# Unread products of the head with 128 columns in place of 256, and the steps of the first fourteen iterations in new places

## The chip, the cores and the metric

The kernel runs on one core of a Trainium2 chip. A core has five engines that work side by side, each from its own queue in strict order: TensorE (PE, matrix products, with a weight load for each), VectorE (DVE), ScalarE (ACT), GpSimd (POOL), and SyncE (SP), whose queue here only starts DMAs. Engines wait for one another by semaphores. The metric is the device time of one execution in microseconds.

## The reference

The reference is one layer of message passing on 128 graphs of 64 nodes with 128 features. For every pair of nodes (i, j) of a graph a three-layer network makes a message of the two nodes' features; the messages are multiplied by the adjacency matrix and summed over j; a second network of the same form updates each node.

```
messages = _mlp(concat[x_i, x_j], msg_w0, msg_b0, ..., msg_w2, msg_b2)   # for all pairs
messages = messages * adj[..., None]
agg      = sum(messages, axis=2)
updated  = x + _mlp(concat[x, agg], upd_w0, upd_b0, ..., upd_w2, upd_b2)
# _mlp: relu(x @ w0 + b0), layer norm, relu(@ w1 + b1), layer norm, @ w2 + b2
```

The adjacency matrix holds zeros and ones, some 12% ones and a full diagonal. So only the pairs with an edge matter.

## The kernel before, in words

The kernel works on edges alone. Each graph gets 640 slots for its edges (five tiles of 128). Two graphs make a pair p (0 to 63), four pairs a block b (0 to 15), two pairs a quad q (0 to 31) with five chunks of 512 edges; chunks are counted by n (0 to 159).

Per block, the place of each edge among the slots is found: `rank` (a scan along each row of the adjacency matrix, DVE), `count` (a product with a triangular matrix, PE), `count_out` and `degrees` (ACT), `place` and `place_out` (POOL; for block 0 `place_first` and `place_pair` on DVE and `place_rest` on POOL). Per pair, `distance` (ACT) and `make_tp` (DVE) mark the slots of each row node, `marks` (PE) and `compare` (DVE) the column node; `node_rows` (ACT for the first six pairs, then POOL) copies the row marks to float32. `stack(p,0)` and `stack(p,1)` are two DMAs each on SP's queue, which put row marks and column marks on top of each other in a tile S[p]. For pairs 0 and 1 no DMA is used: `rows_here` (ACT), `marks_here` (PE) and `compare_here` (DVE) write S directly. `node_marks(p)` is a transposing DMA on SP's queue.

`turn_x`, `turn_x_out`, `rows`, `rows_hi` and `rows_lo` make the first layer's products of each node (transposes and products on PE, copies on ACT, the low part on DVE or POOL).

Per chunk n: `gather(n)` (L946, PE) multiplies those node products by S, so that each edge gets its sum; `relu0(n)` (L951, ACT); `turn_h(n)` (L956, PE, four transposes); `stats0(n)` (L613, DVE); `seed(n)` (ACT or POOL, the second layer's bias times the deviation); `layer1(n)` (L1003, PE); `relu1(n)` (DVE or ACT); `stats1(n)` (DVE). `root_of`, `root1_of`, `inverse_of`, `var1_step` finish the norms per quad, `weights` and `reduce_block` sum the edges into nodes, and the node network follows per block.

gather(n) reads columns 512n to 512n+511 of the slots, so gather(5) is the first to need S[2], gather(7) S[3], gather(15) S[6]. There is one PSUM bank for gather's result, so gather(n+1) waits until relu0(n) is done.

`ahead`, `keep` and unnamed steps derive folded weights once, in the first iterations.

The order of all this is written out by hand. `at(n, place, fn, ...)` files a step under an iteration n and one of sixteen places within it; the table MOVE (lines 24 to 356) overrides that: for a key such as `"gather@@5"` (gather of iteration 5) it gives a shift of the iteration, a new place, and a rank within it. Negative iterations hold the steps of the head, with a running number: `"count@@-1#6"`. At the end all steps run in order of iteration, place and rank, and each step's instructions go to the end of their engines' queues. Changing MOVE therefore changes the order of each engine's queue and nothing else. Tile semaphores follow from the data that steps read and write.

`keep_busy(k)` writes products that nobody reads: `mean_m` against itself (128 columns) k times if k is above 4, else `mean_m` against `first` (256 columns) k // 2 times. It is called with k = 7 once, 4 three times and 2 seven times, so that there are 13 products of 256 columns and 7 of 128. Each float32 product is two records in the trace.

Of the kernel before, what the change touches and what calls it, by code (L numbers as in the profile page):

```python
# [24 lines left out]
    "<lambda>@@1": (1, "s", 1), "<lambda>@@10": (-1, "m", -1), "<lambda>@@11": (0, "T", 2),  # L25
    "<lambda>@@2": (1, "x", 2), "<lambda>@@3": (1, "S1", -1), "<lambda>@@4": (1, "k", 2),
    "<lambda>@@5": (0, "k", 2), "<lambda>@@6": (-1, "S1", -1), "<lambda>@@7": (-1, "T", 2),
    "<lambda>@@8": (0, "k", -5), "<lambda>@@9": (152, "L0", 3), "ahead@@0": (2, "x", 7),
    "ahead@@1": (2, "x1", -1), "ahead@@2": (1, "x1", 0), "ahead@@3": (2, "L1", -1),
    "ahead@@4": (1, "k", 3), "ahead@@6": (0, "T", 2), "bias0.@3": (-7, "a", 2),  # L30
# [3 lines left out]
    "compare.0@7": (0, "m", 0), "compare.0@@0": (2, "x", 6), "compare.0@@10": (2, "e0", 3),  # L34
    "compare.0@@12": (2, "s", 1), "compare.0@@140": (-2, "S1", -1),
    "compare.0@@142": (-2, "k", -1), "compare.0@@145": (-3, "T", 0),
    "compare.0@@147": (-2, "x2", 2), "compare.0@@150": (2, "s", -1),
    "compare.0@@152": (2, "m", -2), "compare.0@@2": (2, "b", 2), "compare.0@@5": (1, "S1", 1),
    "compare.0@@7": (1, "L0", 0), "compare.1@1": (2, "T", -3), "compare.1@3": (3, "y", 2),
    "compare.1@6": (0, "x2", 2), "compare.1@8": (1, "s", 1), "compare.1@@1": (2, "x", 5),  # L40
    "compare.1@@11": (2, "T", -3), "compare.1@@13": (3, "a", 4), "compare.1@@138": (-1, "S1", 1),
    "compare.1@@141": (-2, "T", -1), "compare.1@@143": (-1, "b", 1),
    "compare.1@@146": (-1, "x", 2), "compare.1@@148": (3, "x", 2), "compare.1@@151": (2, "e0", 3),
    "compare.1@@153": (3, "b", 4), "compare.1@@3": (2, "x1", -2), "compare.1@@6": (2, "a", -1),
    "compare.1@@8": (2, "S1", 2), "compare_here@@-1#26": (3, "s", 1),
    "compare_here@@-1#31": (3, "s", 1), "compare_here@@-1#41": (3, "k", 4),
    "compare_here@@-1#47": (3, "x", -1), "count@8": (-2, "e0", -3), "count@@-1#6": (0, "e", -9),
    "count@@1": (1, "k", 5), "count@@138": (-2, "S1", -6), "count@@8": (1, "s", -3),
    "count_out@9": (-3, "e0", -1), "count_out@@-1#7": (0, "e", -9),
    "count_out@@139": (-3, "x", -4), "count_out@@2": (0, "x", 0), "count_out@@9": (0, "e1", 3),  # L50
    "degrees@9": (-6, "T", -2), "degrees@@-1#11": (1, "a", -1), "degrees@@139": (-3, "s", -2),
    "degrees@@2": (0, "s", 2), "degrees@@9": (0, "x1", 0), "distance@0": (-4, "k", -3),
    "distance@3": (1, "k", -1), "distance@5": (-3, "x", -2), "distance@8": (-2, "b", 1),
    "distance@@-1#13": (1, "x2", 0), "distance@@-1#27": (1, "e1", 1),
    "distance@@-1#33": (3, "y", 2), "distance@@1": (1, "k", 4), "distance@@10": (-3, "a", 1),
    "distance@@13": (2, "e", 2), "distance@@138": (-2, "a", -1), "distance@@140": (-3, "s", -1),
    "distance@@143": (-5, "S1", -2), "distance@@145": (-2, "y", 3), "distance@@148": (-7, "k", -1),
    "distance@@150": (-1, "x", 2), "distance@@3": (2, "k", 5), "distance@@5": (1, "y", -3),
    "distance@@8": (0, "x1", -1), "finish.@8": (2, "s", -2), "finish.@@138": (0, "x", -2),
# [7 lines left out]
    "gather@@-1#28": (3, "y", 3), "gather@@-1#35": (3, "x1", -4), "gather@@-1#43": (4, "x", 1),  # L67
    "gather@@0": (3, "e0", 4), "gather@@1": (4, "L1", -5), "gather@@10": (1, "x2", -3),
    "gather@@11": (1, "e0", 3), "gather@@12": (2, "L1", -1), "gather@@13": (2, "e", 2),
# [7 lines left out]
    "gather@@159": (0, "e", 2), "gather@@5": (0, "x1", -1), "gather@@6": (0, "y", -2),  # L77
    "gather@@7": (0, "a", 0), "gather@@8": (0, "k", -6), "gather@@9": (-1, "x1", -1),
# [3 lines left out]
    "inverse_of@@165": (0, "m", 0), "inverse_of@@168": (2, "x2", -1), "keep@@1": (1, "x1", 0),  # L82
    "keep@@10": (0, "L0", 1), "keep@@2": (2, "b", -1), "keep@@3": (2, "L1", -6),
    "keep@@4": (1, "L1", -1), "keep@@5": (0, "k", 3), "keep@@6": (-1, "x1", -1),
    "keep@@7": (1, "s", -2), "keep@@9": (-1, "x1", 3), "keep_busy@@-1#0": (21, "x1", 0),
    "keep_busy@@-1#18": (3, "s", 1), "keep_busy@@-1#23": (17, "x2", -2),
    "keep_busy@@-1#30": (1, "e1", 1), "keep_busy@@-1#37": (17, "T", 2),
    "keep_busy@@-1#45": (3, "s", 1), "keep_busy@@-1#9": (17, "k", -5),
    "keep_busy@@2": (-3, "e", -7), "keep_busy@@3": (-4, "e", -3), "keep_busy@@4": (-5, "e", -7),
    "keep_busy@@5": (-4, "m", -1), "layer1@0": (-3, "m", -1), "layer1@1": (-2, "s", 1),  # L90
    "layer1@2": (-2, "e", 0), "layer1@3": (0, "b", -1), "layer1@4": (2, "m", 3),
    "layer1@5": (1, "y", 0), "layer1@6": (0, "L0", -3), "layer1@7": (-1, "k", -4),
    "layer1@8": (-2, "S1", -7), "layer1@9": (-2, "m", -1), "layer1@@10": (-1, "L1", 1),
    "layer1@@11": (1, "k", 0), "layer1@@12": (1, "e0", 0), "layer1@@13": (1, "L0", 3),
    "layer1@@138": (-2, "S1", -3), "layer1@@139": (-3, "x2", 2), "layer1@@140": (-3, "s", -2),
    "layer1@@141": (-4, "e1", 0), "layer1@@142": (-2, "m", 0), "layer1@@143": (-3, "S1", 2),
    "layer1@@144": (-2, "T", -1), "layer1@@145": (-3, "T", 0), "layer1@@146": (-3, "x", 0),
    "layer1@@147": (-3, "a", 1), "layer1@@148": (0, "a", 0), "layer1@@149": (1, "b", -2),
    "layer1@@150": (-1, "e1", -1), "layer1@@151": (1, "k", 2), "layer1@@152": (1, "T", -3),
    "layer1@@153": (1, "x", -2), "layer1@@154": (1, "m", -1), "layer1@@155": (1, "y", 8),  # L100
    "layer1@@157": (0, "y", -4), "layer1@@158": (0, "a", -2), "layer1@@159": (0, "x2", 1),
    "layer1@@160": (0, "x2", -2), "layer1@@161": (0, "L0", 3), "layer1@@162": (0, "T", -5),
    "layer1@@164": (1, "m", 1), "layer1@@165": (0, "b", 2), "layer1@@166": (0, "e0", 1),
    "layer1@@167": (-1, "m", -2), "layer1@@8": (-2, "e", 0), "layer1@@9": (-1, "k", -5),
    "layer_a.@6": (0, "T", 1), "layer_a.@@146": (3, "x", 2), "layer_a.@@156": (2, "x", -2),
    "layer_a.@@169": (-1, "x1", 0), "layer_a._0@@170": (4, "a", -2),
    "layer_a._2@@171": (7, "L1", 2), "layer_b.@1": (-1, "x1", 1), "layer_b.@@141": (0, "s", 3),
    "layer_b.@@151": (5, "a", 4), "layer_b.@@161": (4, "m", 0), "layer_b.@@171": (5, "y", 2),
    "layer_b._0@@172": (30, "s", 1), "layer_b._2@@173": (30, "s", -1), "layer_c.@7": (-1, "x2", 2),
    "layer_c.@@147": (6, "s", 1), "layer_c.@@157": (4, "s", 1), "layer_c.@@164": (2, "L1", 1),  # L110
    "layer_c.@@173": (30, "L0", 2), "layer_c._0@@174": (39, "x", 0),
    "layer_c._2@@175": (41, "y", -2), "layer_out..uh.m0@7": (-1, "k", -2),
    "layer_out..uh.m0@@147": (2, "e1", 2), "layer_out..uh.m0@@157": (2, "L1", 1),
    "layer_out..uh.m0@@170": (2, "x1", -1), "layer_out..uy.usdb@2": (1, "T", -2),
    "layer_out..uy.usdb@@142": (0, "L0", -4), "layer_out..uy.usdb@@152": (4, "b", 4),
    "layer_out..uy.usdb@@162": (3, "S1", -2), "layer_out..uy.usdb@@172": (5, "L0", -1),
    "layer_out._0.uh.m0@@171": (3, "s", -2), "layer_out._0.uy.usdb@@173": (30, "s", -2),
    "layer_out._2.uh.m0@@172": (7, "a", 2), "layer_out._2.uy.usdb@@174": (30, "k", -1),
    "load_adj@1": (-3, "s", 3), "load_adj@@-1#1": (0, "e", -8), "load_adj@@-1#3": (1, "e1", 2),
    "load_adj@@1": (1, "s", 1), "load_adj@@11": (-6, "a", -2), "load_x@8": (-3, "e0", 3),  # L120
    "load_x@@-1#2": (2, "a", 0), "load_x@@-1#4": (2, "m", -1), "load_x@@138": (-2, "T", -1),
    "load_x@@8": (-6, "x", 7), "make_tp@1": (-4, "m", 0), "make_tp@4": (2, "a", 2),
    "make_tp@6": (-2, "s", 1), "make_tp@9": (-3, "e0", -4), "make_tp@@-1#15": (2, "a", -1),
    "make_tp@@-1#32": (2, "e0", 1), "make_tp@@-1#46": (3, "k", 3), "make_tp@@1": (2, "x", 2),
    "make_tp@@11": (-3, "k", -2), "make_tp@@139": (-3, "x2", 3), "make_tp@@141": (-3, "x1", -3),
    "make_tp@@144": (-5, "k", -1), "make_tp@@146": (-3, "x", 3), "make_tp@@149": (-7, "S1", 1),
    "make_tp@@151": (1, "k", 3), "make_tp@@4": (1, "x1", 0), "make_tp@@6": (0, "k", 2),
    "make_tp@@9": (0, "L0", 4), "marks.0@0": (-1, "x2", 4), "marks.0@2": (2, "L0", 1),
    "marks.0@5": (1, "L0", -1), "marks.0@7": (-1, "e0", 0), "marks.0@@0": (2, "x", 0),
# [230 lines left out]
def tile_gnn(  # L360
# [40 lines left out]
    nc = tc.nc  # L401
# [85 lines left out]
    mean_m = const.tile([P, P], F32, name="mean_m")  # L487
# [1160 lines left out]
```

## Time and profile before

| | us |
|---|---|
| median of five runs | 503.92 |
| lowest and highest | 502.51 and 505.54 |
| the profiled execution | 502.7 |
| its span, first to last instruction | 500.9 |

| engine | busy us | share of the span |
|---|---|---|
| PE | 490.6 | 98% |
| weight loads (beside PE) | 467.6 | 93% |
| DVE | 460.7 | 92% |
| ACT | 398.1 | 79% |
| POOL | 354.3 | 71% |

Busy time of PE counts products from start to modelled end, and neighbours overlap; what a product costs in a full queue is read from the distance of its start to the next start. Idle time in a timeline stands in brackets, with what ended it. SP's rows are issues of DMAs, whose data land later (3.0 us in the median for `stack(p,0)`, 2.7 for `stack(p,1)`).

### The profile page before, as it was taken

Reading aid. Unit: us, or ns where it says so; the run is one execution under the profiler, and the core shown is the slowest. Engines: PE = TensorE matmul, PEld = TensorE weight load, DVE = VectorE, ACT = ScalarE, POOL = GpSimd, SP = SyncE. Lnnn points to the kernel's source line nnn. Section 1 sums busy time; section 2 is a strip of 40 time slices with the busy share of each in tenths; the row PEclk is TensorE's granted clock in tenths of the full one; section 3 lists DMA queues with packets and bytes.
Section 4 is the critical chain, followed back from the end, with each engine's and each line's share of the span. In section 5 each row is a group of like instructions: output and inputs, shape, how many; then the busy total and the mean of one; then the engine's idle time right before and its main releaser. Section 6 shows DMA issues by size and latency. Waiting matters only on the chain.

```text
span 500.9 us, 15934 instructions
## 1 busy us (share of the span) xinstructions
PE 490.6 (98%) x5969; PEld 467.6 (93%) x5969; DVE 460.7 (92%) x1225; ACT 398.1 (79%) x907; POOL 354.3 (71%) x563
## 2 busy tenths in 40 slices
PE   7999999999999999999999999999999999999995
PEld 5899999999999999999999999999999999999984
DVE  7899788999999999999999999899999989998885
ACT  6999978888787788968778897877879778867753
POOL 3277686877869687785968778696886669674941
PEclk9999999999999999999999999999999999999999
DMA  4769475658849575694956667475565647355201
GB/s 122 167 145 171 105 139 120 132 121 141 167 105 151 119 148 121 139 165 106 151 127 135 135 130 162 98 168 128 121 150 117 152 110 170 85 114 107 63 23 46
DMA packets 91474, 63.55 MB, mean 127 GB/s; under 512 B 57473, under 2 KB 75522, under 8 KB 91394
## 3 DMA queue, kind: packets, MB, share of 16 engines
q1 hardware_dynamic: 91106, 62.36, 58.9%
q8 instruction: 49, 0.80, 0.7%
q14 instruction: 31, 0.25, 0.2%
q10 hardware_dynamic: 288, 0.13, 0.1%
HBM read 7.15 MB, written 4.19 MB: 23 GB/s over the span
## 4 chain that ended last, share of the span: by engine, by line


## 5 line engine op out<-in xcount | busy, mean ns | idle before, releaser
L1003 PE MATMUL z<-w1c,h 128*128 128x128 f32 x1280 | 167.4, 275 | 0.0
L1003 PEld LDWEIGHTS z<-w1c,h 128*128 128x128 f32 x1280 | 158.1, 191 | 4.1
L613 DVE BATCH_NORM_STATS2 st<-hT 128x6 f32<-128x256 f32 x320 | 120.5, 418 | 21.6 <-PE hT L956 17.7
L951 ACT ACTIVATE h<-hps,b0c 128x512 f32<-128x512 f32 x160 | 109.6, 685 | 23.9 <-PE hps L946 22.7
L993 ACT ACTIVATE z<-b1b,m_sd 128x128 f32<-128x128 f32 x320 | 118.8, 371 | 11.6 <-DVE y L597 4.7
L613 DVE BATCH_NORM_STATS2 st<-y 128x6 f32<-128x256 f32 x320 | 118.1, 419 | 0.1
L989 POOL TENSOR_TENSOR u<-b1b,m_sd 128x512 f32<-128x512 f32 x80 | 82.8, 1044 | 29.4 <-ACT m_sd L621 28.9
L956 PE MATMUL hT<-ident,h 128*128 128x128 f32 x640 | 96.5, 273 | 0.7 <-ACT h L951 0.6
L946 PE MATMUL hps<-s,abl 128*128 128x512 f32 (+3 forms) x256 | 93.5, 371 | 0.8 <-DMA s<-j 0.5
L1045 POOL TENSOR_TENSOR w<-oh,m_q 128x192 f32<-128x192 f16 x126 | 62.6, 511 | 39.8 <-issue 27.0
L956 PEld LDWEIGHTS hT<-ident,h 128*128 128x128 f32 x640 | 74.3, 141 | 1.9 <-ACT h L951 1.0
L946 PE MATMUL hps<-s,abh 128*128 128x512 f32 (+3 forms) x256 | 74.3, 322 | 0.0
L1012 ACT ACTIVATE y<-z 128x512 f32<-128x512 f32 x80 | 47.4, 595 | 30.9 <-PE z L1003 30.7
L928 DVE TENSOR_TENSOR j<-mk,cmpt 128x320 fp32r<-128x320 f32 x124 | 58.4, 471 | 1.4 <-PE mk L920 1.2
L597 DVE CUSTOM_DVE_ANT_0 y<-z,u 128x512 f32<-128x512 f32 x80 | 54.0, 675 | 4.0 <-PE z L1003 2.4
L889 ACT ACTIVATE d<-slot,mid 128x640 f16<-128x640 f16 x64 | 52.7, 826 | 0.7 <-DVE mid L799 0.7
L946 PEld LDWEIGHTS hps<-s,abl 128*128 128x128 f32 x256 | 48.7, 190 | 2.8 <-DMA s<-j 0.7
L946 PEld LDWEIGHTS hps<-s,abh 128*128 128x128 f32 x256 | 48.5, 189 | 0.0
L1060 PE MATMUL ys<-y,w 128*32 128x128 f32 x1488 | 44.3, 274 | 0.0
L1060 PEld LDWEIGHTS ys<-y,w 128*32 128x32 f32 x1488 | 39.7, 110 | 3.6 <-POOL w L1045 2.6
L904 POOL CAST i<-tp 128x640 fp32r<-128x640 f16 x58 | 42.4, 746 | 0.0
L920 PE MATMUL mk<-tp,posall 128*128 128x320 f16 x126 | 37.9, 300 | 0.2 <-DVE j L928 0.2
(195 smaller groups left out, 852.2 us busy)
## 6 DMA issues: line engine op xcount, KB each, us to landing
s<-i SPq DMA_DIRECT2D x124, 160.0 KB, 3.0
s<-j SPq DMA_DIRECT2D x124, 160.0 KB, 2.7
xn<-in_x_dram SPq DMA_DIRECT2D x15, 256.0 KB, 4.0
out_dram<-uo SPq DMA_DIRECT2D x15, 256.0 KB, 2.5
an<-in_adj_dram SPq DMA_DIRECT2D x16, 128.0 KB, 2.7
oh<-tp SPq DMA_TRANSPOSE x64, 3.1
xn<-in_x_dram SPq DMA_DIRECT2D x2, 128.0 KB, 3.2
out_dram<-uo SPq DMA_DIRECT2D x2, 128.0 KB, 3.5
```

What stands on the lines that cost most here:

```text
L597: nc.vector._custom_dve(TENSOR_ADD_SAT, out=o, in0=ps, in1=sb, s0=BIG, s1=0.0)
L613: nc.vector.bn_stats(st, src.rearrange("p t c -> p c t"))
L889: nc.scalar.activation(D[p], slot, AF.Abs, bias=blocks[b]["mid"][:, q:q + 1], scale=-1.0)
L928: nc.vector.tensor_tensor(JR[p][:, c], MK.pop((p, k))[:, 0:HC], cmpt[:, c], op=ALU.is_equal)
L946: nc.tensor.matmul(ps[:, c:c + w], lhsT=ab[:, g % 4, :], rhs=s, start=(k == 0), stop=(k == 1))
L951: nc.scalar.activation(H[n], HP.pop(n), AF.Relu, bias=b0c)
L956: nc.tensor.transpose(ps[:, t, :], H[n][:, t * P:(t + 1) * P], ident)
L989: nc.gpsimd.tensor_tensor(U[n], bc(W["b1b"], CH), SR[q][:, k:k + CH].unsqueeze(2).to_broadcast([P, CH, C]), op=ALU.mult)
L993: nc.scalar.activation(z_of(n)[:, t, :], W["b1b"], AF.Copy, scale=SR[q][:, k + t:k + t + 1])
L1003: nc.tensor.matmul(ps[:, t, :], lhsT=h[:, t * P:(t + 1) * P], rhs=W["w1c"], start=added and t == 0, stop=True, skip_group_check=True)
L1045: (nc.vector if p == NP - 2 else nc.gpsimd).tensor_tensor(WT[p][:, g], oh, qs, op=ALU.mult)
L1060: nc.tensor.matmul(YS[b][g * N + m * HN:g * N + (m + 1) * HN, k, :], lhsT=w[:, g, m, u, :], rhs=y, start=(u == 0), stop=(u == TH - 1), til ...
```

## The change

Two things are changed. `keep_busy` uses 128 columns always, with the number of products as it was (13 and 7). And the entries of MOVE for the head and for iterations 0 to 13 have new values (some 570 positions of 2,983 in the order differ, nearly all before the step gather(19); of those behind it, keep_busy(7) and root_of(3) change places, and a step that issues no instruction moves). No step is added or removed.

```
-            if k > 4:
-                for _ in range(k):
-                    nc.tensor.matmul(warm[:, 0, :], lhsT=mean_m, rhs=mean_m, start=True, stop=True)
-            else:
-                for _ in range(k // 2):
-                    nc.tensor.matmul(warm[:, 0:2, :], lhsT=mean_m,
-                                     rhs=first.rearrange("p q j -> p (q j)"), start=True,
-                                     stop=True)
+            for _ in range(k if k > 4 else k // 2):
+                nc.tensor.matmul(warm[:, 0, :], lhsT=mean_m, rhs=mean_m, start=True, stop=True)
```

```
 MOVE = {
...
-    "compare.1@@11": (2, "T", -3), ...
+    "compare.1@@11": (4, "a", 2), ...
-    "count@@-1#6": (0, "e", -9),
+    "count@@-1#6": (1, "s", -1),
-    "keep_busy@@-1#0": (21, "x1", 0), "keep_busy@@-1#18": (3, "s", 1), "keep_busy@@-1#23": (17, "x2", -2),
-    "keep_busy@@-1#30": (1, "e1", 1), "keep_busy@@-1#37": (17, "T", 2), "keep_busy@@-1#45": (3, "s", 1),
-    "keep_busy@@-1#9": (17, "k", -5), "keep_busy@@2": (-3, "e", -7), "keep_busy@@3": (-4, "e", -3),
-    "keep_busy@@4": (-5, "e", -7), "keep_busy@@5": (-4, "m", -1),
+    "keep_busy@@-1#0": (21, "x1", 1), "keep_busy@@-1#18": (1, "y", 4), "keep_busy@@-1#23": (17, "e1", -2),
+    "keep_busy@@-1#30": (1, "e1", -3), "keep_busy@@-1#37": (17, "T", 1), "keep_busy@@-1#45": (2, "e1", -2),
+    "keep_busy@@-1#9": (1, "b", 0), "keep_busy@@2": (2, "k", 0), "keep_busy@@3": (-3, "s", -1),
+    "keep_busy@@4": (0, "s", -1), "keep_busy@@5": (11, "k", -5),
-    "node_marks@@9": (0, "x1", 4), "node_marks@@10": (-4, "e1", 3),
+    "node_marks@@9": (-5, "x1", -1), "node_marks@@10": (-5, "k", 10),
-    "node_rows@@10": (2, "e0", 4),
+    "node_rows@@10": (5, "e0", 3),
-    "stack.0@@11": (3, "x1", -1), "stack.1@@12": (4, "m", 5),
+    "stack.0@@11": (5, "L1", -2), "stack.1@@12": (3, "e0", 2),
...
```

The order that follows, from the first step to the step gather(5):

```
before
load_adj(0); rank(0); keep_busy(2); keep_busy(2); odd_weights(0); count(0); keep_busy(2); count_out(0); place_first(); degrees(0); distance(0); distance(1); keep_busy(4); load_adj(1); place_pair(0); make_tp(0); load_x(0); turn_x(0,0,2); rank(1); load_x(1); keep_busy(2); marks_here(0); turn_x_out(0,0,2); make_tp(1); rows_here(0,0); place_rest(); turn_x(0,2,4); load_adj(2); rows(0,0,0,2); keep_busy(4); compare_here(0,0); compare_here(0,1); keep_busy(2); turn_x_out_rest(); degrees(1); rows_hi(0,0,0,2); marks_here(1); distance(2); rows_lo(0,0,0,2); gather(0); make_tp(2); distance(3); rows(0,0,2,4); rows_here(0,1); relu0(0); compare_here(1,0); count(1); rows_hi(0,0,2,4); compare_here(1,1); turn_h(0); count_out(1); marks(2,0); rows_lo(0,0,2,4); compare(2,0); load_x(2); rows_here(1,0); ahead(); gather(1); keep(); stats0(0); marks(2,1); relu0(1); node_rows(2); rows_here(1,1); turn_h(1); gather(2); ... stack(2,0); stack(2,1); ... stack(3,0); compare(3,1); stack(3,1); gather(5)
after
load_adj(0); rank(0); odd_weights(0); degrees(0); load_adj(1); count(0); count_out(0); keep_busy(2); place_first(); distance(0); distance(2); keep_busy(2); load_x(0); place_pair(0); make_tp(0); keep_busy(4); turn_x(0,0,2); turn_x_out(0,0,2); distance(1); rank(1); marks_here(0); compare_here(0,0); rows(0,0,0,2); ahead(); turn_x(0,2,4); make_tp(1); rows_hi(0,0,0,2); rows_lo(0,0,0,2); rows_here(0,0); load_adj(2); keep_busy(4); turn_x_out_rest(); rows_here(0,1); compare_here(0,1); make_tp(2); place_rest(); gather(0); marks_here(1); relu0(0); rows(0,0,2,4); compare_here(1,0); distance(3); count(1); count_out(1); rows_hi(0,0,2,4); compare_here(1,1); gather(1); degrees(1); relu0(1); marks(2,0); rows_here(1,0); rows_here(1,1); compare(2,0); keep_busy(2); place(1); rows_lo(0,0,2,4); turn_h(0); gather(2); stats0(0); ... compare(2,1); ... load_x(2); gather(3); stack(2,1); ... node_rows(2); ... keep_busy(2); ... gather(4); ... keep_busy(2); ... relu0(4); ahead(); stack(2,0); node_marks(0); node_rows(3); ... node_marks(1); gather(5)
```

Further on, up to gather(15):

```
before
... node_rows(6); node_rows(7); ... stack(7,0); ... stack(6,0); ... node_marks(2); ... load_x(3); ... gather(13); ... stack(6,1); ... gather(15)
after
... seed(6); ... place_out(2); ... node_marks(2); ... stack(6,1); ... load_x(3); node_rows(6); ... stack(6,0); stack(7,0); ... gather(15)
```

In both versions the four products of keep_busy(4), keep_busy(2) and keep_busy(2) that stand in iteration 16, and keep_busy(7) in iteration 20, stay about where they were.

## The prediction

> **What bounds the kernel now.** I read the page first (engine sums, slices), then a table of busy time by stretch of time, then the timelines of TensorE (PE), ScalarE (ACT), VectorE (DVE) and of SP's queue up to 62 us, where the change lies.
>
> ```profile
> span 500.9 us, 15934 instructions
> PE 490.6 (98%) x5969; PEld 467.6 (93%) x5969; DVE 460.7 (92%) x1225; ACT 398.1 (79%) x907; POOL 354.3 (71%) x563
> ```
>
> ```profile
> 10.00:20.00 10.00, 9.35 (x100) 7.32 (x100) 9.51 (x26) 9.84 (x22) 2.81 (x6) 1.00 0.57 134
> 20.00:30.00 10.00, 9.52 (x99) 8.56 (x98) 8.29 (x22) 9.17 (x21) 5.17 (x5) 1.00 0.77 179
> 30.00:40.00 10.00, 10.00 (x126) 9.35 (x128) 9.95 (x25) 9.84 (x27) 6.88 (x11) 1.00 0.92 164
> 40.00:54.00 14.00, 14.00 (x146) 12.86 (x139) 12.94 (x36) 13.39 (x30) 9.02 (x20) 1.00 0.56 129
> 100.00:200.00 100.00, 100.00 (x1207) 97.07 (x1207) 95.85 (x255) 81.21 (x183) 76.67 (x116) 1.00 0.67 134
> ```
>
> The columns are length, then busy time and count of PE, weight loads, DVE, ACT, POOL. From 100 us on ACT is idle 19% of the time and PE never: PE is the bound there. In the head it is different: from 30 to 54 us ACT (9.84 of 10, 13.39 of 14) is as full as PE. So the reader is to see that a saving in the head counts only as far as ACT moves up too.
>
> The timelines say where the head loses time (start, length, engine, line, what it does; idle time in brackets):
>
> ```profile
> 5.43 1.55 ACT L889 ACTIVATE d<-slot,mid 128x640 f16<-128x640 f16 x2 [0.74 <-DVE mid L799]
> 7.47 0.37 ACT L838 COPY xnT<-hT 128x256 f32<-128x256 f32 x1 [0.49 <-PE hT L832]
> ...
> 22.37 0.69 ACT L951 ACTIVATE h<-hps,b0c 128x512 f32<-128x512 f32 x1 [0.67 <-PE hps L946]
> ...
> 53.09 0.69 ACT L951 ACTIVATE h<-hps,b0c 128x512 f32<-128x512 f32 x1
> ```
>
> ```profile
> 1.91 2.07 PE L1329 MATMUL ys<-first,mean_m 128*128 128x256 f32 x4 [1.91 <-DVE first L505]
> 4.17 2.91 PE L1329 MATMUL ys<-first,mean_m 128*128 128x256 f32 x6
> ...
> 8.86 1.56 PE L1329 MATMUL ys<-first,mean_m 128*128 128x256 f32 x6
> ...
> 47.75 1.08 PE L1329 MATMUL ys<-first,mean_m 128*128 128x256 f32 x4
> ...
> 53.86 0.50 PE L946 MATMUL hps<-s,abl 128*128 128x512 f32 x1
> ```
>
> ACT's rows sum to 2.47 us of idle between 4.3 and 55 us: 0.74, 0.49, 0.13, 0.07, 0.07, 0.67, 0.13, 0.17. The last gather of the changed stretch starts at 53.86, right after relu0(18) ends on ACT (53.09 + 0.69 = 53.78): at its end the head is paced by ACT. The unread products show the clock: six records take 2.91 us at 4.17 and 1.56 us at 8.86, so PE ran at about half rate until some 7.2 us, 5.3 us after its first product.
>
> **Unread products, 13 of them, 128 columns for 256.** Each is two records. At full rate the 256-column record costs (1.08 - 0.38)/3 = 0.23 us of PE, the 128-column one 1.61/14 = 0.115 us (the seven of keep_busy(7) fill 59.33 to 60.94). So 13 x 2 x 0.115 = 3.0 us of PE work go. But nine stood before the first gather (10.44), where PE waits anyway. Four stand at 47.75 to 53.37 in both versions: 0.92 + 0.43 + 0.48 = 1.83 us become 0.92. Three of the moved ones now stand behind the first gather: +0.69. PE gains 0.2 us net, and that in a stretch that ACT paces: counted as nothing. Without that cover it is 0.9 us.
>
> **Steps moved: ACT.** Every step up to iteration 16 stays in the head, so each engine's work there is unchanged: ACT's must still pass between 4.34 us and relu0(18). What can go is its idle time. Of the eight gaps the first, 0.74 (the chain rank, count, place_first), stays. distance(2) now stands ahead of turn_x_out(0) and fills the 0.49. The 0.67 stood before relu0(5), because gather(5) waited for stack(2,1); that stack now goes out right after compare(2,1), and stack(2,0) after node_rows(2), which comes 23 places ahead of relu0(4). ACT's rows before 22.37, gaps left out, run at 0.87 of the sum of their lengths (neighbours overlap); at that pace node_rows(2) ends near 17 us in the new order and its DMA (3.0 us to landing) near 20, when relu0(4) ends too, so the wait is gone. With the small gaps 0.13 + 0.07 + 0.07: 1.43 us less.
>
> **Steps moved: DVE.** DVE is full from 3.40 to 12.5 us, and the rows queued in front of compare_here(1,0) sum to the same 7.54 us in both orders (two ranks, odd_weights, place_first, place_pair, three make_tp, four compares, rows_lo). So it starts at 10.7 in both. Later DVE has 0.88 + 0.49 idle (before stats0(4) and stats0(5)), about what ACT gains: no term. make_tp(7) and (9) took 1.09 and 1.18 us against 0.37 elsewhere, and may shrink or others grow in new places; DVE's slack takes that.
>
> **Steps moved: the clock.** Before, two unread products stand in front of count and three right behind it; now count is PE's first instruction, at 4.14, and two 128-column products follow, then two more, then turn_x: about 2.1 us of work at half rate, then PE idles about a microsecond until make_tp(0) has ended (7.2 in both). No row shows when the clock opens now. Lower end: at 7.2 as before, cost 0 (a gain is excluded, PE starts no earlier). Nearest row: 5.3 us after the first product, 9.5; then rows(0,0), 0.57 us at full rate, takes 1.15 in front of rows_hi, for which ACT waits: 0.5. If the pause voids what came before it, 5.3 us count from 7.3 and the clock opens at 12.6. The products from marks_here(0) to turn_h(0) take 4.6 us at full rate (marks 0.27 + 0.27 + 0.14, rows 0.57 + 0.57, turn_x 0.43, gathers 0.56 + 0.63, unread 0.69, count 0.03, turn_h 0.44), so turn_h(0) would end at 11.9 instead of 12.8 before; half of 5.3 us lost makes it 14.55, 1.75 later than before. If the clock stays shut through turn_h(0), 7.3 + 9.2 = 16.5: 3.7 later. I take 0.5, the nearest row; ends 0 and 3.7.
>
> [...]
>
> **Steps moved: DMAs and POOL.** SP's queue is strict. node_marks(0) and (1) (1.31 and 1.38 us of SP each) now stand before stack(3,*): gather(7) wants S[3] at about 25.3, and the queue lands it at about 25.5, a wait of 0.2 in front of relu0(7), which ACT reaches only at 26: nothing. load_adj(3) and load_x(2) are hidden (blocks needed 8 us later). POOL: seed(3) and place(2) now precede rows_lo(1,0), which ends near 31.2, gather(10) wants it near 32: hidden by 0.8.
>
> Late next is S[6], for gather(15), needed near 44.1 to 45 (45.18 before). Before, stack(6,0) issued at 36.5. Now node_rows(6) stands behind seed(6) and place_out(2) on POOL, and stack(6,0) behind stack(6,1) and load_x(3) on SP:
>
> ```profile
> 39.12 1.80 SPq L737 DMA_DIRECT2D xn<-in_x_dram  x1
> 41.02 1.10 SPq L911 DMA_DIRECT2D s<-j  x2
> ```
>
> stack(6,1) needs compare(6,1), now behind four statistics: DVE near 39.5. Then 1.1 for it, 0.4 to 1.8 for load_x(3), 0.55 to the second half of stack(6,0), 3.0 to land: 44.6 to 46.5. gather(15) waits 0 to 1.8 us; behind it on PE stand layer1(8) and turn_h(14), on ACT relu0(15). I take 0.8, the middle.
>
> **Sum.** -1.43 (ACT's gaps) + 0.5 (clock) + 0.8 (S[6]) + 0 = -0.1 us on the profiled execution: 502.7 (span 500.9 and 1.8 around it) becomes 502.6. The five runs spread from 502.51 to 505.54 with median 503.92, 1.2 above the profiled one; for a median I forecast 503.8. 0.5% (2.5 us) is about what a measurement of this kernel can tell from no change.
>
> **Rivals.**
> [...]
> *Stacks late* (slower). SP issues of 2.4 to 2.8 us for a pair are in the trace (2.48 at 28.59). If stack(6,0) takes that as well, S[6] lands near 48, 3.5 us late: -1.43 + 0.5 + 3.5 = +2.6, 506.5. Against: DMA engines are busy only 56% of 40 to 54 us.
> *All gaps close* (faster). ACT loses 1.43 + 0.13 + 0.17 = 1.73, S[6] and clock are in time, and the 0.9 us of narrower products at 47 to 53 counts: 503.9 - 2.6 = 501.3. Against: gather(19) waits for ACT, which has no 0.9 to give.
> *The change does not do what it says*: a product of 128 columns could cost as much as one of 256, if weight loads set its time. The rows exclude it (0.115 against 0.23).
>
> **How the numbers follow.** Forecast 0.56 (its own range 502.5 to 505.7, from 0 to 1.8 for S[6] and 0 to 1.75 for the clock), clock late 0.18, stacks late 0.10, all gaps close 0.16. So faster 0.16, same 0.56, slower 0.28. The range for 8 in 10 reaches to both outer cases, 501.4 to 507.2.
>
> **What would show it.** Right: no ACT wait before turn_x_out(0) nor relu0(5); compare_here(1,0) at 10.7 to 11.2; gather(15) idle for a DMA by less than 1.8 us; gather(19) within 1 us of 53.9. Wrong: records of 128 columns spaced 0.21 us after 11 us (clock); gather(15) after 47 (stacks); gather(19) before 52 (gaps), or a time that differs though gather(19) does not.

## The result, and the profile after

The changed kernel is slower by 0.23%: median 504.17 us over 38 runs (503.05 to 506.64) against 503.0 for the kernel before over 67 runs (501.57 to 506.02), ratio 1.0023 with a 95% interval of 1.0014 to 1.0031. That is 1.2 us more, where the prediction said 0.1 us less. The time lies inside the stated range of 501.4 to 507.2, but the direction is wrong.

The profiled execution of the changed kernel took 504.99 us (span 503.0), 2.3 above the profiled one of before. The page of the changed kernel, its span and its busy times:

```profile
span 503.0 us, 15941 instructions
PE 489.2 (97%) x5969; PEld 466.5 (93%) x5969; DVE 460.9 (92%) x1225; ACT 398.7 (79%) x907; POOL 352.4 (70%) x563
```

PE is busy for 1.4 us less, and the span is 2.0 longer (502.96 for 500.92). Busy time by stretch of the changed kernel (length, then PE, weight loads, DVE, ACT, POOL):

```profile
10.00:20.00 10.00, 9.89 (x97) 7.38 (x96) 8.49 (x24) 9.05 (x21) 2.69 (x6) 1.00 0.48 113
20.00:30.00 10.00, 9.33 (x97) 8.43 (x98) 8.67 (x24) 9.32 (x23) 3.76 (x7) 1.00 0.84 182
30.00:40.00 10.00, 10.00 (x107) 9.21 (x106) 9.74 (x26) 9.76 (x23) 5.46 (x7) 1.00 0.50 116
40.00:54.00 14.00, 12.81 (x152) 11.67 (x152) 12.36 (x31) 12.51 (x29) 10.86 (x20) 1.00 0.72 159
100.00:200.00 100.00, 100.00 (x1219) 96.88 (x1208) 95.74 (x254) 80.94 (x182) 78.01 (x117) 1.00 0.70 140
```

Two stretches have changed. From 10 to 20 us ACT and DVE, the pacing engines, fell from 9.84 and 9.51 to 9.05 and 8.49, and PE is fuller (9.89 for 9.35) though it issues fewer matmuls (97 for 100): it runs slower. From 40 to 54 us all three fell: PE from 14.00 to 12.81.

Where the difference arises is seen from the starts of the gathers (from the instruction timelines of both, us):

| step | before | after | later by |
|---|---|---|---|
| gather(0) | 10.44 | 10.13 | -0.31 |
| gather(3) | 16.53 | 17.60 | 1.07 |
| gather(5) | 21.60 | 22.24 | 0.64 |
| gather(14) | 43.38 | 44.53 | 1.15 |
| gather(15) | 45.18 | 47.72 | 2.54 |
| gather(19) | 53.86 | 56.12 | 2.26 |
| gather(60) | 174.34 | 176.66 | 2.32 |
| gather(120) | 350.93 | 353.26 | 2.33 |

Nothing is gained or lost from gather(19) on until the last blocks. Between gather(5) and gather(14) the same work stands in another order, so single rows there cannot be compared (gather(13) is even 0.96 earlier). What remains are two steps: about 1.1 us in the first 17 us, and 1.4 at gather(15).

The first one is the clock. The timeline of PE in the changed kernel, early (start, length; what it waited for in brackets):

```profile
4.17 0.17 PE L752 MATMUL ma<-rk,lt 128*128 128x4 f16 x1 [4.17 <-DVE rk L743]
4.20 2.06 PE L1324 MATMUL ys<-mean_m 128*128 128x128 f32 x8
...
7.30 0.43 PE L919 MATMUL mk<-tp,posall 128*128 128x320 f16 x1 [0.62 <-DVE tp L894]
...
9.42 1.06 PE L1324 MATMUL ys<-mean_m 128*128 128x128 f32 x4
10.13 0.78 PE L945 MATMUL hps<-s,abl 128*128 128x512 f32 x1
...
12.89 0.67 PE L945 MATMUL hps<-s,abl 128*128 128x384 f32 x1
13.36 0.41 PE L945 MATMUL hps<-s,abh 128*128 128x384 f32 x1
```

The first half of gather(0) takes 0.78 us where it took 0.50, that of gather(1) still 0.67. In the trace's record of the granted clock the stretch at full rate begins at 7.23 us in the kernel before and at 13.51 here. Ahead of that PE runs at about half rate: eight unread records of 128 columns take 0.23 us each (4.20 to 6.04), for 0.115 at full rate.

What became of ACT's gaps, in ACT's timeline of the changed kernel:

```profile
5.46 1.55 ACT L888 ACTIVATE d<-slot,mid 128x640 f16<-128x640 f16 x2 [0.82 <-DVE mid L798]
6.91 0.35 ACT L837 COPY xnT<-hT 128x256 f32<-128x256 f32 x1
...
9.07 0.37 ACT L868 CAST abh<-mu 128x256 fp32r<-128x256 f32 x1 [0.67 <-PE mu L846]
...
11.38 0.69 ACT L950 ACTIVATE h<-hps,b0c 128x512 f32<-128x512 f32 x1 [0.30 <-PE hps L945]
13.07 0.26 ACT L757 ACTIVATE raw<-ma,mid_c 128x4 f32<-128x4 f32 x1 [0.29 <-PE ma L752]
13.97 0.69 ACT L950 ACTIVATE h<-hps,b0c 128x512 f32<-128x512 f32 x1 [0.28 <-PE hps L945]
...
23.24 0.70 ACT L950 ACTIVATE h<-hps,b0c 128x512 f32<-128x512 f32 x1
...
28.27 0.69 ACT L950 ACTIVATE h<-hps,b0c 128x512 f32<-128x512 f32 x1 [0.57 <-PE ma L752]
...
48.46 0.69 ACT L950 ACTIVATE h<-hps,b0c 128x512 f32<-128x512 f32 x1 [0.82 <-PE hps L945]
...
55.38 0.69 ACT L950 ACTIVATE h<-hps,b0c 128x512 f32<-128x512 f32 x1
```

The two large gaps that were to close have closed: turn_x_out(0) at 6.91 and relu0(5) at 23.24 have no wait. But new ones stand elsewhere: before rows_hi (9.07), relu0(0), count_out(1) and relu0(1), before relu0(7) (28.27) and relu0(15) (48.46). relu0(18), the last row, starts 2.29 later than before.

The waits before relu0(7) and relu0(15) come from PE, and PE's from stacks. (For relu0(7) the profile names the product that stands right behind gather(7) on PE.) PE's timeline and SP's queue of the changed kernel there:

```profile
27.75 0.36 PE L945 MATMUL hps<-s,abl 128*128 128x256 f32 x1 [0.66 <-DMA s<-j]
...
47.72 0.47 PE L945 MATMUL hps<-s,abl 128*128 128x512 f32 x1 [1.12 <-ACT z L992]
```

```profile
20.05 2.67 SPq L1033 DMA_TRANSPOSE oh<-tp  x2
22.83 0.52 SPq L728 DMA_DIRECT2D an<-in_adj_dram  x1
23.45 1.10 SPq L910 DMA_DIRECT2D s<-i  x2
24.65 1.19 SPq L910 DMA_DIRECT2D s<-j  x2
...
41.12 2.37 SPq L910 DMA_DIRECT2D s<-j  x2
43.54 0.59 SPq L736 DMA_DIRECT2D xn<-in_x_dram  x1
44.23 2.46 SPq L910 DMA_DIRECT2D s<-i  x4
```

The second half of gather(7) waits 0.66 for S[3]: stack(3,1) goes out at 24.65, behind the two node_marks and load_adj(3). gather(15) waits 1.12 at 47.72; the profile names an ACT step that had long ended, and what came last is S[6]: the first part of stack(6,0) is issued at 44.23 and has landed 3.4 us later, at 47.6. In SP's queue stack(6,1) takes 2.37 us where a pair mostly takes 1.1; one of its two issues lasted 1.87.

### The profile page after: what moved, and what is told of

It is laid out like the page before. It is cut to its first block, busy times and chain, and to the rows that moved or that the text cites. A ratio compares the mean times of both kernels' runs of the same rounds, so it can differ in the third digit from the quotient of the medians.

```text
span 503.0 us, 15941 instructions
## 1 busy us (share of the span) xinstructions
PE 489.2 (97%) x5969; PEld 466.5 (93%) x5969; DVE 460.9 (92%) x1225; ACT 398.7 (79%) x907; POOL 352.4 (70%) x563
## 4 chain that ended last, share of the span: by engine, by line
```

## The experiments

Each kernel ran beside the kernel before (medians 502.75 to 503.13), and the ratio is against those. Lags are starts against the profiled execution of before, in us.

| run | median us | ratio to before | 95% interval | clock opens | gather(3) lag | gather(15) lag | gather(19) lag |
|---|---|---|---|---|---|---|---|
| the change | 504.17 | 1.0023 | 1.0014 to 1.0031 | 13.51 | 1.07 | 2.54 | 2.26 |
| width_alone | 502.72 | 0.9997 | 0.9986 to 1.0007 | 13.25 | 1.15 | 0.44 | 0.29 |
| order_alone | 504.63 | 1.0036 | 1.0024 to 1.0049 | 7.07 | 0.08 | 0.77 | 0.85 |
| s6_early | 503.77 | 1.0009 | 0.9995 to 1.0022 | 13.11 | 0.92 | 1.09 | 1.08 |
| warm_early | 502.69 | 0.9997 | 0.9986 to 1.0007 | 9.05 | 0.02 | -0.02 | -0.14 |
| warm_s6 | 502.76 | 0.9999 | 0.9984 to 1.0014 | 8.68 | -0.03 | -0.03 | -0.06 |
| warm_s3 | 502.47 | 0.9990 | 0.9972 to 1.0008 | 9.72 | 0.17 | 0.17 | -0.10 |
| before_s2 | 501.75 | 0.9975 | 0.9960 to 0.9990 | 5.99 | -0.03 | -0.86 | -0.86 |
| late4 | 502.65 | 0.9996 | 0.9982 to 1.0011 | 6.15 | -0.27 | -0.81 | -0.96 |
| narrow_s2 | 502.55 | 0.9989 | 0.9971 to 1.0007 | 12.37 | 0.98 | 0.26 | 0.11 |
| best | 502.09 | 0.9978 | 0.9964 to 0.9992 | 8.61 | 0.70 | 0.08 | -0.07 |
| best_warm | 501.23 | 0.9974 | 0.9960 to 0.9987 | 4.03 | -0.19 | -0.98 | -1.13 |
| after_again | 503.89 (one run) | | | 10.31 | 0.06 | 1.14 | 0.87 |

The columns of clock and lags are from one profiled execution each; the median is over 9 to 12 runs.

### The two halves of the change: width_alone and order_alone

width_alone is the kernel before with its own MOVE and the new keep_busy:

```
-            if k > 4:
-                for _ in range(k):
-                    nc.tensor.matmul(warm[:, 0, :], lhsT=mean_m, rhs=mean_m, start=True, stop=True)
-            else:
-                for _ in range(k // 2):
-                    nc.tensor.matmul(warm[:, 0:2, :], lhsT=mean_m,
-                                     rhs=first.rearrange("p q j -> p (q j)"), start=True,
-                                     stop=True)
+            for _ in range(k if k > 4 else k // 2):
+                nc.tensor.matmul(warm[:, 0, :], lhsT=mean_m, rhs=mean_m, start=True, stop=True)
```

> The kernel before with its own order; only the thirteen unread products are 128 columns wide in place of 256. Three theories. Order theory (the loss of 1.2 us is made by the new places, by late stacks of S[6] above all): the width does nothing, 503.0 within 0.4, gather(15) starts at 45.2 as before. Clock theory (the loss comes from PE staying at half rate until 13.5 us instead of 7.2): the narrower products leave pauses of about 1 us in front of count and of place_pair, the clock opens after 9 us, and the time is 0.5 to 1.2 above before, with the lag already there at gather(3). Cover theory (narrower products free 0.9 us of PE at 47.75 to 53.37): 0.5 to 0.9 below before.

Measured: no difference that shows. But its profile is not that of a kernel where nothing happened: the clock opens at 13.25, gather(3) is 1.15 late, as the clock theory had it, and from gather(5) on only 0.45 of that is left. ACT no longer waits before relu0(5):

```profile
22.27 0.59 ACT L838 COPY xnT<-ma 128x512 f32<-128x512 f32 x1
22.81 0.69 ACT L951 ACTIVATE h<-hps,b0c 128x512 f32<-128x512 f32 x1
```

In the order of before, ACT's 0.67 of idle time ahead of relu0(5) was there to be used up: S[2], for which gather(5) waits, does not follow the clock (the last issue of stack(2,1) ended at 19.36 here and at 19.74 before), so a late start was free up to that length.

order_alone has the new MOVE and the old keep_busy with 256 columns.

> The changed order with the products of before (256 columns). Order theory: as the changed kernel, 1.2 above before, gather(15) idle for a DMA by about 1.1 as there. Clock theory: wider products fill the stretch from 4.2 us, which puts off turn_x by 0.9 but opens the clock nearer to 9.5 than 13.5; gather(3) then starts before 17.6 and the time is 0.3 to 0.8 above before, not 1.2. Cover theory: 0.9 more PE work at 47 to 53 us, so 1.5 to 2.1 above before.

Measured: 504.63, 1.8 us (1.2 to 2.5) above before. So the new order alone loses, and the new width does not add to that; the change as a whole is 0.5 (medians) to 0.7 (ratios) lower, but the two intervals overlap. In this profile the clock opened at 7.07 and gather(3) was in time, and still gather(15) was 0.77 and gather(19) 0.85 late. A late clock is then not the whole loss. ACT waits 0.81 before turn_x_out(0), behind the wider products (0.49 in before), and 0.42 before relu0(7), and gather(15) waits for S[6]:

```profile
7.86 0.37 ACT L837 COPY xnT<-hT 128x256 f32<-128x256 f32 x1 [0.81 <-PE hT L831]
```

```profile
45.95 0.47 PE L945 MATMUL hps<-s,abl 128*128 128x512 f32 x1 [0.48 <-DMA s<-i]
```

That the median is worse than this profiled execution (503.91) may be due to other openings of the clock; this was not measured.

### The late S[6]: s6_early

```
-    "node_rows@@10": (5, "e0", 3),
+    "node_rows@@10": (2, "x", 1),
...
-    "stack.0@@11": (5, "L1", -2),
+    "stack.0@@11": (3, "y", 1),
```

> The changed kernel with two steps put forward: node_rows(6) right behind node_rows(7) (POOL is idle there) and stack(6,0) right behind stack(5,1), so that stack(6,0) is issued at about 35 in place of 44.2; stack(6,1) stays. Order theory (S[6] late): gather(15) starts at 46.3 to 46.8 in place of 47.7 without a wait for a DMA, and the time falls by 1.0 to 1.4, to that of before. Clock theory (the head is late by its first 14 us, and this late start carries through whatever waits later): gather(15) moves but gather(19) stays near 56, and the time falls by less than 0.4.

Measured: gather(15) starts at 46.27 without a wait for S[6], gather(19) 1.18 earlier than in the changed kernel, and the time falls by 0.4 (medians) to 0.7 (ratio 1.0009 for 1.0023). PE's row:

```profile
46.27 0.48 PE L945 MATMUL hps<-s,abl 128*128 128x512 f32 x1
```

The order theory's mechanism is right, the size is about half of what it expected, and the intervals of the two kernels overlap.

### The late clock: warm_early

```
-    "keep_busy@@2": (2, "k", 0), "keep_busy@@3": (-3, "s", -1),
+    "keep_busy@@2": (-2, "y", 6), "keep_busy@@3": (-4, "e", 2.5),
...
-        for n, k in ((2, 2), (3, 2), (4, 2), (5, 2)):
+        for n, k in ((2, 4), (3, 5), (4, 2), (5, 2)):
```

> The changed kernel with the first unread products in other places and numbers: five of 128 columns ahead of count (from 1.9 to 4.1 us, where PE waits anyway) and two behind turn_x(0,0,2) (where PE is idle for 0.6), taken from behind count and from iteration 4. Clock theory: the clock opens at 7 to 8 us, gather(3) starts at 16.3 to 16.8 in place of 17.6, gather(8) at 28.6 or earlier in place of 29.8, and the time falls by 0.8 to 1.3. Order theory: the early stretch gains, but gather(15) still waits for S[6], whose chain (compare(6,1), stack(6,1), load_x(3), stack(6,0)) follows the clock only in part: the time falls by 0.5 at most.

Measured: 502.69, that is 1.3 us below the changed kernel (ratios 0.9997 and 1.0023) and level with before. The clock opened at 9.05, later than was written, but gather(3) came at 16.55 and gather(8) at 28.51, as written. PE's timeline of this run:

```profile
1.05 2.50 PE L1324 MATMUL ys<-mean_m 128*128 128x128 f32 x10 [1.05 <-DVE eps_c L489]
4.18 0.17 PE L752 MATMUL ma<-rk,lt 128*128 128x4 f16 x1 [0.62 <-DVE rk L743]
4.20 1.63 PE L1324 MATMUL ys<-mean_m 128*128 128x128 f32 x6
```

gather(15) lost its wait too: stack(6,1) was issued 1.3 earlier (39.85) and took 1.10 in place of 2.37, and stack(6,0) went out at 41.68, 2.5 earlier than in the changed kernel. SP's queue of this run:

```profile
39.85 1.10 SPq L910 DMA_DIRECT2D s<-j  x2
40.99 0.59 SPq L736 DMA_DIRECT2D xn<-in_x_dram  x1
41.68 2.46 SPq L910 DMA_DIRECT2D s<-i  x4
```

### Both at once: warm_s6

The edits of warm_early and of s6_early together.

> The changed kernel with both repairs: the early unread products of the run before (five of 128 columns ahead of count, two behind turn_x(0,0,2)), and node_rows(6) and stack(6,0) put forward. If the late clock and the late S[6] are two losses beside each other, their gains of 1.3 and 0.7 add up: 1.8 to 2.0 below the changed kernel, 0.5 to 0.8 below the kernel before. If S[6] was late only because the start was late (with the early products gather(15) already starts at 45.16, as before), nothing is added: the time of the run with the early products alone, within 0.3.

Measured: 502.76, nothing beyond warm_early. The two gains do not add; in the profiled execution of warm_early S[6] is in time, and its repair has nothing to repair.

### A second look at the change: after_again

The changed kernel, not edited.

> The changed kernel once more, unchanged, for a second profiled execution. If the clock opens at 13.5 by the order of the work alone, it opens there again within 0.3, and the time is 504.5 to 505. [...]

Measured: the clock opened at 10.31, and the execution took 503.89, 1.1 less than the first profiled one. gather(3) is 0.06 late and gather(14) 0.12 early: in this execution the early loss is gone without any edit. What stays is S[6]. PE's timeline and SP's queue of this run:

```profile
46.32 0.47 PE L945 MATMUL hps<-s,abl 128*128 128x512 f32 x1 [1.02 <-DMA s<-i]
```

```profile
39.84 2.08 SPq L910 DMA_DIRECT2D s<-j  x2
41.96 0.59 SPq L736 DMA_DIRECT2D xn<-in_x_dram  x1
42.66 2.44 SPq L910 DMA_DIRECT2D s<-i  x4
```

stack(6,1) starts at the same time as in warm_early and takes 1.0 longer; everything behind it is late by that, and gather(15) waits 1.02. At gather(3), gather(8) and gather(14) the two executions agree within 0.04, although the clock opened 1.3 later here (10.31 for 9.05); what separates them is this one issue. Whether the early products shorten it, or chance does, these single executions do not show. The loss of the change so has two parts that come and go: the clock's, by when it opens, and that of S[6], by how long one issue lasts.

### Is a closed gap worth its length: before_s2 and warm_s3

before_s2 is the kernel before with two loads that are not urgent moved behind S[2] on SP's queue:

```
-    "load_adj@@11": (-6, "a", -2),
+    "load_adj@@11": (-6, "k", 3.6),
...
-    "load_x@@8": (-6, "x", 7),
+    "load_x@@8": (-3, "k", 3.5),
```

> The kernel before, with load_x(2) and load_adj(3) behind stack(2,1) on SP's queue in place of ahead of stack(2,0), so that both parts of S[2] are issued some 0.7 earlier. It closes alone one of the gaps that the forecast counted: ACT's 0.67 before relu0(5). If a closed gap of ACT in the head is worth its length: gather(5) at 21.1 or earlier in place of 21.6, gather(19) near 53.3, the time 0.4 to 0.7 below before. If not, gather(19) stays at 53.9 within 0.15 and the time too.

Measured: 501.75, ratio 0.9975 (0.9960 to 0.9990). SP's queue and relu0(5) on ACT in this run:

```profile
14.88 2.30 SPq L911 DMA_DIRECT2D s<-i  x2
17.28 1.18 SPq L911 DMA_DIRECT2D s<-j  x2
18.50 0.59 SPq L737 DMA_DIRECT2D xn<-in_x_dram  x1
19.19 0.51 SPq L729 DMA_DIRECT2D an<-in_adj_dram  x1
```

```profile
20.99 0.59 ACT L838 COPY xnT<-ma 128x512 f32<-128x512 f32 x1
21.52 0.69 ACT L951 ACTIVATE h<-hps,b0c 128x512 f32<-128x512 f32 x1
```

stack(2,1) goes out at 17.28 in place of 18.56, the wait before relu0(5) is gone, and the lag goes from -0.11 at gather(4) to -0.83 at gather(5) and stays there to gather(19). This closed gap of ACT was worth its full length: 0.72 between gather(4) and gather(5), for 0.67. The time fell by more than was written, 1.3 us by the ratio, with 0.5 to 2.0 as its interval; this profile accounts for 0.9 of it. The gap also differs from execution to execution: in late4 below, which does not move these loads, gather(5) was 0.80 early, 0.44 of it gained since gather(4), in an execution where an issue of stack(2,0) was shorter.

warm_s3 adds to warm_early a repair of the wait before relu0(7):

```
-    "node_marks@@9": (-5, "x1", -1), "node_marks@@10": (-5, "k", 10), "load_adj@@11": (-6, "x", 4),
+    "node_marks@@9": (-3, "T", 1), "node_marks@@10": (-4, "T", 2), "load_adj@@11": (-5, "T", 3),
```

> The kernel with the early unread products, and node_marks(0), node_marks(1) and load_adj(3) behind stack(3,1) on SP's queue in place of ahead of stack(3,0) and stack(3,1). With the early products ACT still idles 0.42 before relu0(7), because gather(7) waits for S[3]. If an idle stretch of ACT in the head is worth its length: stack(3,1) is issued at about 22 in place of 23.2, the wait is gone, gather(19) starts near 53.3 and the time falls by 0.3 to 0.5 against the run with the early products alone. If what follows swallows it (the next wait, S[4] or compare(4,0), takes its place): no change, within 0.15 at gather(19).

Measured: 502.47, 0.2 below warm_early and not to be told from it, gather(19) in the same place (-0.10 for -0.14). The wait before relu0(7) is gone (0.42), and 0.41 stands in front of relu0(10) in its place, as PE's and ACT's timelines of this run show:

```profile
32.78 0.47 PE L945 MATMUL hps<-s,abl 128*128 128x512 f32 x1 [0.35 <-DMA s<-j]
```

```profile
33.53 0.69 ACT L950 ACTIVATE h<-hps,b0c 128x512 f32<-128x512 f32 x1 [0.41 <-PE hps L945]
```

gather(10) is the first to read S[4], and S[4] was next to be late. This closed gap was worth nothing that shows, because the next stack was late in its place.

### What the gap was worth to a late clock: narrow_s2

The edits of width_alone and before_s2 together: the clock opens late, and the loads are out of the way of S[2].

> The kernel before with all thirteen unread products narrow (as in the run of the width alone, whose clock opened at 13.25) and S[2] issued earlier (as in the run that moved load_x(2) and load_adj(3)). In the run of the width alone the late clock cost 1.15 at gather(3) and only 0.44 from gather(5) on. If that was because the gap of 0.67 before relu0(5) swallowed the rest: with the gap closed the lag stays near 1 through gather(5), gather(19) starts at 53.9 to 54.3 and the time is 0.6 to 1.0 above the run that closes the gap with wide products (501.75). If the late clock costs the same in either order: 0.3 above that run, gather(19) at 53.2 to 53.4.

Measured: the clock opened at 12.37. Against before_s2 gather(3) is 1.01 later, gather(5) 1.09, gather(16) 1.12, and the time 0.8 more (502.55 for 501.75; the intervals of the two ratios overlap). relu0(5) has no wait on ACT:

```profile
22.08 0.59 ACT L838 COPY xnT<-ma 128x512 f32<-128x512 f32 x1
22.62 0.69 ACT L951 ACTIVATE h<-hps,b0c 128x512 f32<-128x512 f32 x1
```

In the order of before, where the gap exists, the late clock cost 1.15 at gather(3) and only 0.44 at gather(16) (width_alone). So in these executions the late clock was cheap only as long as a wait behind it could shrink. The change closed that wait and delayed the clock in one edit.

### The width where PE is full: late4

Only the four products at 47.75 to 53.37 are narrow, in the kernel before:

```
+        asked = []
         def keep_busy(k):
-            if k > 4:
-                for _ in range(k):
+            asked.append(k)
+            if k > 4 or len(asked) > 7:
+                for _ in range(k if k > 4 else k // 2):
```

> The kernel before, in which only the four unread products at 47.75 to 53.37 us are 128 columns wide (those of the start stay at 256). It measures the term that the forecast put at nothing. If ACT covers it: gather(19) at 53.86 within 0.1, the time of before within 0.2. If PE has no cover there: 0.9 of PE's time goes, gather(19) near 53.0 and the time 0.6 to 0.9 below before. The run with all thirteen narrow lost 0.15 of its lag between gather(16) and gather(19), which points to 0.1 to 0.2.

Measured: 502.65, the time of before within its interval. The term itself is read from the starts: the lag is -0.82 at gather(16), -1.26 at gather(17), -0.93 at gather(18), -0.96 at gather(19). PE gains 0.44 at once, most of it is taken back by gather(18), where ACT paces, and 0.14 remains. The 0.8 ahead of gather(16) has nothing to do with the edit: in this execution the clock opened 1.1 earlier (0.27 at gather(3)), and the first issue of stack(2,0) took 1.39 where it took 2.16 in the profile of before.

### A version that beats both: best and best_warm

best has the edits of before_s2 and late4. best_warm moreover replaces the two wide products ahead of count by seven narrow ones:

```
-        for n, k in ((2, 2), (3, 2), (4, 2), (5, 2)):
+        for n, k in ((2, 7), (3, 2), (4, 0), (5, 2)):
```

> The kernel before with the two edits that gained: S[2] issued earlier, and the four unread products at 47.75 to 53.37 us narrow. If the gains add (0.87 at gather(19) by the first, of which 0.1 was an earlier clock, and 0.11 from gather(16) to gather(19) by the second): gather(19) at 52.8 to 53.0, the time at 501.5 to 501.7, ratio 0.997. If the second is swallowed: as the first alone, 501.75.

> The run with both gains, and in place of the two wide products ahead of count seven narrow ones, which do not read the tile first and can start at 1.05 in place of 1.91. If the clock opens after a stretch without pauses: at 5 to 6.5 us, and the time falls by up to 0.3. If narrow products count for less, or the pauses weigh more: it opens at 8 us or later, and the time rises by 0.2 to 0.5.

best: 502.09, ratio 0.9978; faster than before, not to be told from before_s2. Its profiled execution is no proof of the sum, since its clock opened at 8.61 and gather(3) was 0.70 late. best_warm: 501.23, ratio 0.9974 (0.9960 to 0.9987). Its clock opened at 4.03, and ten of its twelve runs lie between 500.98 and 501.55. It beats both kernels of this study; against before_s2 (0.9975) and best its advantage is not shown.

## Why the prediction was wrong, point by point

ACT's idle time up to relu0(18) accounts for most of the lag in the first execution of the changed kernel, and for about half of it in the second. The terms, in us, worked out from the gaps in ACT's timelines:

| term | predicted | first execution | second execution |
|---|---|---|---|
| gaps that close (0.49, 0.13, 0.07, 0.07, 0.67) | -1.43 | -1.43 | -1.43 |
| the other 0.13, before relu0(14), closes too | 0 | -0.13 | -0.13 |
| clock: before rows_hi | 0.5 | 0.67 | 0.67 |
| clock: before relu0(0), count_out(1), relu0(1) | 0 | 0.87 | 0 |
| S[3] for gather(7) | 0 | 0.57 | 0.39 |
| S[6] for gather(15), and relu0(16) behind it | 0.8 | 1.01 | 0.91 |
| first gap, 0.82 for 0.74 | 0 | 0.08 | 0.08 |
| sum of the gaps | -0.13 | 1.64 | 0.49 |
| rest of relu0(18)'s lag | 0 | 0.65 | 0.41 |
| relu0(18) later by | -0.1 | 2.29 | 0.90 |

**Which step failed.** The costs set against the closed gaps were too small: the clock, taken at 0.5 from the nearest row, and the terms put at nothing, S[3] and the overlap of neighbouring rows. In the first execution the clock is the largest miss, 1.54 for 0.5. In the second, whose time (503.89) is nearer to the median (504.17), it is 0.67 for 0.5, and S[3] with 0.39 and the rest with 0.41 are the larger misses. warm_early shows the same with a clock much as forecast (9.05 for 9.5) and with S[6] in time: the prediction's terms then sum to -0.93, and relu0(18) was only 0.11 early. ACT waited 0.67 before rows_hi there, and 0.42 for S[3]:

```profile
26.98 0.69 ACT L950 ACTIVATE h<-hps,b0c 128x512 f32<-128x512 f32 x1 [0.42 <-PE ma L752]
```

**The gaps that close.** Right: all five are gone, though before rows_hi 0.67 stands where 0.13 stood.

**The clock.** The nearest row (5.3 us from the first product) was taken, and the clock should have opened at 9.5; it opened at 13.51 and 10.31. The row came from an order in which PE has hardly a pause in this stretch (0.16 us in front of count); the new order has 0.62 in front of marks_here(0). The other reading, that the pause voids what came before it and the clock opens at 12.6, is not borne out either: behind the pause at 6.7 to 7.3 the clock still took 3.0 and 6.2 us, not 5.3. The price of the early part, 0.5 before rows_hi, was about right (0.67). The part above it, up to 0.87, was left out of the forecast and held only in its range. The 0.18 for a late clock, and with it the range's upper end of 507.2, stand for a still later opening, which no run shows: the latest was at 13.51, and the slowest of the 38 runs took 506.64.

**S[3].** Wrong: counted as 0.2 and hidden, measured as 0.57 and 0.39 of ACT's time. On SP the two node_marks and load_adj(3) hold the queue from 20.05 to 23.35, stack(3,1) goes out at 24.65 and its first part is there at 27.6, not at 25.5. The 0.67 that left relu0(5) came back in good part at relu0(7). The prediction asked "what is late next" for S[6] and not for S[3], the very next stack. Nor is S[3] the end of it: warm_s3 took its wait away, and S[4] was late in its place.

**S[6].** Mechanism, place and size right (0.8 predicted, 0.9 to 1.0 measured), gather(15) idle by 1.12 and 1.02, under the limit of 1.8. It started after 47 in the first execution because everything ahead of it was late as well.

**The rest** of 0.65 and 0.41 is for the most part not idle time. ACT's steps ahead of relu0(18) are 102 rows with the same sum of lengths (52.71 us in before and in the first execution, 52.77 in the second), but neighbours overlap by 6.35 us in place of 7.08 (6.72 in the second execution). Idle times too short for the table add 0.13 and 0.16, and the first row starts 0.2 and 0.1 earlier. The prediction used one share, 0.87, for both orders; measured it is 0.866 before and 0.880 and 0.873 after.

**The unread products.** Counting them at nothing was right for PE's time, and ACT was the cover: late4 shows 0.44 gained and 0.14 kept. What the prediction missed is their other effect. In the order of before, narrow products leave pauses ahead of count and behind the early products (2.03 and 0.62 us in narrow_s2, 0.16 and none in before), and the clock opens at 13.25 and 12.37 in place of 5.99 to 8.61. In the new order it opened at 10.31 to 13.51 with narrow products and at 7.07 with wide ones, and the wide ones were no faster, since they hold up turn_x.

**DVE.** compare_here(1,0) started at 11.67 and 11.33, not at 10.7 to 11.2: the rows queued ahead of it sum to 7.70 us before and 7.73 after, the same in both orders as was said, though not 7.54. But it also waits for marks_here(1) on PE, which the slow clock delays (0.42 us idle in the first execution, none in the second), and in both executions rows_lo, one of the rows ahead, waited 0.30 for rows_hi.

**The sum.** The forecast took the gain of closed gaps and the cost of the clock as two independent terms. width_alone and narrow_s2 show that they are not: with the gap, a late clock cost 0.44 at gather(16); without it 1.12. The upper end of the forecast's own range, 505.7, is also too low for its terms: 1.75 for the clock and 1.8 for S[6] less 1.43 are 2.1, which gives 506.0.

Not settled: why one issue of stack(6,1) takes 1.57 to 1.87 in three runs of the new order (0.95 in order_alone), and 0.60 in the three with early products. Single long issues stand in other places of every head, that of before too (load_x(3), 1.80). Since warm_early removed both causes at once, the share of each in the 1.2 us of the medians is known only roughly: S[6] 0.4 to 0.7 by s6_early (with overlapping intervals), the rest the clock, S[3] and the smaller overlap on ACT.

## What to carry to other kernels

A wait in the head is also a buffer: before you close it, ask which earlier delay it swallows, and do not add such a delay in the same edit. When a gap closes because a transfer goes out sooner, look at the next transfer on the same queue first; here the gain was kept when loads that were not urgent went behind the urgent one (0.25%), and lost when the next stack was just as late. The unread products of the head did best here when they started as early as their operands allow and left no pause up to the opening (from 1.05, opening at 4.03 in best_warm); their width mattered less for what it costs (0.14 kept in late4) than for the pauses it left (2.03 in narrow_s2, opening at 12.37).

## What the runs showed of the hardware

The record of the granted clock in fourteen profiled executions has three lengths for the stretch at full rate: 484.69 us, 488.11 (the first execution of the changed kernel) and 491.52 (that of before), which are 3.41 or 3.42 apart. It opens at anything from 4.03 (best_warm) to 13.51.

The same changed kernel opened at 13.51 and at 10.31. In both executions PE begins with count (4.17 and 4.22), waits 0.62 before marks_here(0) (until 7.30 and 7.35) and starts gather(0) at 10.13 and 10.18, so the order of the work alone does not set the opening. The first half of gather(0) takes 0.78 in the first and 0.54 in the second. The 3.2 us more of half rate went with 1.0 us at gather(3) (1.07 and 0.06 late). What sets the moment of the opening is not shown by these runs.
